# Conditioned mixture of experts and ternary feed-forward on one core: dense experts in two blocks of eight, expert-sorted tokens through DRAM in the other six

## The chip, the cores and the metric

The kernel runs on one core of a Trainium2 chip. The metric is the device time of one launch in microseconds (us). The core has TensorE (PE; its weight loads are shown apart as PEld), VectorE (DVE), ScalarE (ACT), GpSimd (POOL) and SyncE (SP), which here only issues DMAs. Each engine works through its own instructions in the order in which the program was written, and waits on semaphores for the others.

## The reference

4096 tokens (B = 128 rows of S = 32) of width D = 128. Cut to what matters:

```python
U = (mu @ W_dec + b_dec).reshape(B, IN_DIM + 1, K)          # K = 30, one matrix per row of the batch
param = einsum('bik,kj->bij', U, V)                         # rank 30
out = einsum('bsd,bde->bse', x, param[:, :-1]) + param[:, -1:]
gate = out @ Wg.T + bg                                      # 8 experts
topk_scores, topk_idx = top_k(gate, 2);  w = softmax(topk_scores)
h = gelu(einsum('td,ehd->teh', out, W1) + b1)               # H = 256 for each expert
o = einsum('teh,eoh->teo', h, W2) + b2
x = x + (the two chosen experts' o, weighted with w)
c = conditioning(x, ids, states)   # layernorms with table look-ups, one more layer, layernorm
h = silu(tlin(c, w1) * w1_s) * (tlin(c, w2) * w2_s)         # 128 -> 512, weights in {-1, 0, 1}
h = gelu(tlin(h, h1) * h1_s);  h = gelu(tlin(h, h2) * h2_s) # 512 -> 512, twice
x = x + tlin(h, w3) * w3_s                                  # 512 -> 128
```

Only two of the eight experts enter the sum of a token. `out` has rank 30 before the experts, so a token can be carried as 30 numbers and a one (KZ = 32), and the kernel folds V into W1.

## The kernel before, in words

The tokens are cut into eight blocks of TB = 512 (NB = 8). Weights lie in SBUF from the start. PSUM has five kinds of 128x512 tile: `tp` (two), `mm` (two), `ff` (two), `bc` and `acc` (one each).

**Setup.** L184 makes the per-row matrices, `conditioned(i)` (L221) a block's 32 numbers per token (`z4s[i]`, split into two float32r halves), L206 and L207 fold V into W1 (`w4`), L308 computes the gates of all blocks, and `routing` (L252) finds the best two experts by reductions on DVE, and writes their weights as rows (`hot4`, last written in L301).

**`experts(i)`** (L473) runs all eight experts over all 512 tokens of a block. After four transposes of `hot4` (L480) and the bias product (L487), each expert has one matmul that spreads its weights over the partitions (`pbc`, L491), and twice: first layer (`ph`, L495, float32r), gelu on ACT (`hs`, L497), product with the weights on DVE (`hw`, L499) and second layer (`po`, L500, float32, which the profile shows as two matmul records each). Then x is added (L505) and the block is stored to DRAM (`kept_x`, L506) for the case at the end.

**`conditioning(i)`** (L511) is a serial chain: transposes (L522), layernorm x, transposes (`pxh`), table look-ups as matmuls (L542), layernorm h, three products with tables (L559), transposes, five matmuls into `pi` (L576 to L580), a tanh, one more layer (L594, L596), layernorm c, transposes, result `cT`, stored to DRAM (L609). A layernorm (L394) has its statistics and its scaling on DVE and between them two small POOL operations: add eps (L402) and power -0.5 (L403). For layernorm h the scaling itself (L405) is on POOL.

**`feed_forward(i)`** (L631) multiplies in float32r with each activation split into two halves by `halves` (L617): `hi` a cast on ACT (L620), `lo` a subtraction on POOL (L622). Four steps of the gated layer (`pf`; ACT L627, DVE L628 and L629), four of `pgb`, four of `pgc` (matmuls L638, gelu L666), the last layer `pf`, then x is added (L677), four transposes (L680), a copy (L682) and the store.

**Other streams.** `feed_forward_weights` (L360) loads the ternary weights in eleven pieces into five buffers (`ffr`), casts each on ACT, compares on DVE (L368) and sums on POOL (`unequal`, L369) whether a cast changed anything; `count_unequal` puts the sum into a register, and the general path behind it (L748, L749) runs only if it isn't zero. `second_layer_weights` (L422) runs three small state networks, each with a layernorm (`rs_st`).

**Order.** All are generators, and the order in which instructions are written is the order on every engine. `beside` (L51) mixes streams by their share done; L735 to L744 give the stages:

```python
    beside((experts(0), 18), (feed_forward_weights(), 11), (second_layer_weights(), 8))
    count_unequal()
    beside((conditioning(0), 13), (experts(1), 18))
    for i in range(NB):
        streams = [(feed_forward(i), 14)]
        if i + 1 < NB:
            streams.append((conditioning(i + 1), 13))
        if i + 2 < NB:
            streams.append((experts(i + 2), 18))
        beside(*streams)
```

So six stages hold feed-forward i, conditioning i+1 and experts i+2; the seventh has no experts, the eighth is feed-forward 7 alone.

Of the kernel before, what the change touches and what calls it, by code (L numbers as in the profile page):

```python
# [30 lines left out]
VPW = 125  # L31
EPS = 1e-5
# [18 lines left out]
def beside(*streams):  # L51


    left = [[s, n, 0] for s, n in streams]
    while left:
        e = min(left, key=lambda e: (e[2] + 0.5) / e[1])
        e[2] += 1
        if next(e[0], e) is e:
            left.remove(e)
# [3 lines left out]
def adaln_ffn_kernel(ctx: ExitStack, tc: tile.TileContext, a, out: bass.AP):  # L63
# [32 lines left out]
    def rows(tag, n):  # L96

        t = const.tile([P, n], F32R, tag=tag, name=tag)
        nc.gpsimd.memset(t.bitcast(F32), 0.0)
        return t  # L100
# [12 lines left out]

    early = ctx.enter_context(ExitStack())
    setup = early.enter_context(tc.tile_pool(name="setup", bufs=1))
# [10 lines left out]
    x_all = setup.tile([D, NB, TB], F32, tag="x_all", name="x_all")  # L126
    for i in range(NB):
        nc.sync.dma_start(x_all[:, i, :], a["x_t"][:, i * TB : (i + 1) * TB])
    tabs = load("tabs", [4 * E, NTAB], eng=nc.scalar, pool=setup)
    vecs = load("vecs", [P, NVEC], eng=nc.scalar)  # L130
    w2_t = load("moe_w2", [P, E, NH, D])
# [24 lines left out]
    def stacked(dst, src, r, tmp):  # L156
# [3 lines left out]
        hi = tmp.tile([n, dst.shape[1]], F32R, tag="hi", name=f"hi_{dst.tensor.name}", bufs=2)  # L160
# [8 lines left out]
    twice = const.tile([2 * KZ, 2, 2 * KZ], F32R, tag="twice", name="twice")  # L169
# [30 lines left out]
    w4 = const.tile([P, E * H], F32R, tag="w4", name="w4")  # L200
    g4 = const.tile([P, E], F32R, tag="g4", name="g4")

    def folded(dst, w, bias, name):
        n = dst.shape[1]
        pv = ps_acc(name)
        nc.tensor.matmul(pv[:, :n], pre[:, V4 : V4 + P], w, start=True, stop=False)  # L206
        nc.tensor.matmul(pv[:, :n], bias_at, bias, start=False, stop=True)  # L207
        stacked(dst, pv[:, :n], 64, setup)

    def folded_all():  # L210
        folded(g4, pre[:, WG : WG + E], bias_rows[:, E * H :], "pgv")
        yield
        for c in range(E * H // TB):
            cols = slice(c * TB, (c + 1) * TB)
            folded(w4[:, cols], w1_t[:, cols], bias_rows[:, cols], f"pwv_{c}")
            yield


    z4s = [const.tile([P, TB], F32R, tag=f"z4_{i}", name=f"z4_{i}") for i in range(NB)]

    def conditioned(i):  # L221
        xT = x_all[:, i, :]
# [9 lines left out]
        zT = setup.tile([KZ, TB], F32, tag="zT", name=f"zT_{i}", bufs=2)  # L232
# [6 lines left out]
        zh = setup.tile([2 * KZ, TB], F32R, tag="zh", name=f"zh_{i}", bufs=2)  # L239
# [607 lines left out]
```

## Time and profile before

| what | us |
|---|---|
| median of three runs (565.28 to 568.62) | 567.3 |
| the profiled execution | 565.48 |
| its span (first to last instruction) | 563.4 |
| `pwT` of block 0 begins (setup done) | 63.4 |
| x1T of block 0 is stored | 102.1 |
| the output of block 0 is stored | 196.75 |
| outputs of blocks 1 to 5 are stored | 253.25, 309.73, 366.24, 422.75, 479.01 |
| output of block 6 | 522.2 |
| last matmuls of block 7 | 558.4 |

The span is 2.1 us below the profiled execution's time, which is 1.8 us below the median. A stage with three streams takes 56.5 us. All DMAs are issued from the queues of SP and ACT; POOL issues none. The mean granted clock of TensorE is 0.942.

How to read it: the page's first part gives the busy time of each engine, its second part cuts the span into 40 slices of 14.1 us, and its groups give for a line of code how often it ran, the mean of one, and how long its engine sat idle before it and for whom. The table of windows gives the same busy times for stretches of the span, with the clock that was granted to TensorE.

### The profile page before, as it was taken

The page shows a single profiled execution, that of the slowest core. Times are in us where ns is not written, and L with a number is a line of the kernel's source. Part 1 is how long each engine was busy: PE and PEld are TensorE (multiplying, and loading weights), DVE is VectorE, ACT ScalarE, POOL GpSimd, SP SyncE. Part 2 cuts the span into 40 slices and gives each one's busy share as a digit, 9 for nine tenths or more (in the row PEclk, how much of TensorE's full clock was granted, in tenths as well). Part 3 has the DMA queues.
Part 4 walks back from the last instruction along what each step waited for, and adds up shares of the span by engine and source line. Part 5 has one row for each costly group of instructions (what it writes and reads, how often), then busy time and mean ns, then how long its engine had stood idle before and what let it go on. Part 6 is the DMA issues. An engine that isn't in the chain of part 4 may idle for free. (4 is left out here: it accounts for less than half of the span.)

```text
span 563.4 us, 5941 instructions
## 1 busy us (share of the span) xinstructions
PE 497.5 (88%) x1997; PEld 310.3 (55%) x1997; DVE 289.0 (51%) x689; ACT 235.4 (42%) x412; POOL 209.4 (37%) x226
## 2 busy tenths in 40 slices
PE   5998587979899979997999799979997999689694
PEld 5963243534566546654665466546654665365373
DVE  2875786744763565356535653565356535623400
ACT  0141553322455344534453455345534552353343
POOL 3000065030373237323722372237223722384353
PEclk9985599989899999999999999999999999899588
DMA  8800330100100020002000200020001000100100
GB/s 209 298 11 3 113 110 1 39 19 5 53 19 2 2 74 19 0 3 74 19 1 3 74 19 0 5 74 18 1 1 57 0 1 1 56 0 1 37 0 24
DMA packets 14634, 20.46 MB, mean 36 GB/s; under 512 B 1632, under 2 KB 7358, under 8 KB 14342
## 3 DMA queue, kind: packets, MB, share of 16 engines
q1 hardware_dynamic: 13762, 19.56, 10.9%
q10 hardware_dynamic: 836, 0.47, 0.4%
q8 instruction: 18, 0.29, 0.2%
q14 instruction: 18, 0.14, 0.1%
HBM read 13.72 MB, written 6.29 MB: 36 GB/s over the span
## 5 line engine op out<-in xcount | busy, mean ns | idle before, releaser
L500 PE MATMUL po<-hw,moe_w_sb 128*128 128x512 f32 x256 | 135.8, 627 | 8.7 <-DVE hw L499 8.7
L499 DVE TENSOR_TENSOR hw<-hs,pbc 128x512 f32<-128x512 f32 x128 | 85.9, 681 | 67.7 <-PE pbc L491 35.0
L497 ACT ACTIVATE hs<-ph 128x512 f32<-128x512 f32 x128 | 74.6, 596 | 55.2 <-PE ph L495 31.8
L622 POOL TENSOR_TENSOR gc_lo<-gc,gc_hi 128x512 fp32r<-128x512 f32 x32 | 40.7, 1273 | 95.8 <-ACT gc_hi L620 95.2
L500 PEld LDWEIGHTS po<-hw,moe_w_sb 128*128 128x128 f32 x256 | 44.2, 193 | 48.4 <-DVE hw L499 36.5
L622 POOL TENSOR_TENSOR ga_lo<-ga,ga_hi 128x512 fp32r<-128x512 f32 x32 | 41.0, 1280 | 68.9 <-ACT ga_hi L620 68.9
L495 PE MATMUL ph<-z,w 128*128 128x512 f32 x128 | 53.2, 442 | 2.5 <-ACT hs L497 2.5
L622 POOL TENSOR_TENSOR gb_lo<-gb,gb_hi 128x512 fp32r<-128x512 f32 x32 | 40.5, 1287 | 18.8 <-ACT gb_hi L620 16.6
L638 PE MATMUL pgc<-gb_lo,f_h_hi 128*128 128x512 f32 x128 | 44.8, 454 | 1.4 <-POOL gb_lo L622 1.3
L638 PE MATMUL pgb<-ga_hi,f_h_hi 128*128 128x512 f32 x128 | 42.7, 447 | 1.3 <-DVE sl L628 1.3
L666 ACT ACTIVATE gb<-pgb,vecs_sb 128x512 f32<-128x512 f32 x32 | 22.0, 689 | 50.1 <-PE pgb L638 50.1
L638 PE MATMUL pgc<-gb_hi,f_h_hi 128*128 128x512 f32 x128 | 41.0, 437 | 0.1
L666 ACT ACTIVATE gc<-pgc,vecs_sb 128x512 f32<-128x512 f32 x32 | 22.0, 689 | 45.4 <-PE pgc L638 45.4
L627 ACT ACTIVATE sl<-pf,half_w1s 128x512 f32<-128x512 f32 x32 | 22.0, 688 | 43.8 <-PE pf L638 41.1
L638 PE MATMUL pf<-cT_hi,f_w_hi 128*128 128x512 f32 x64 | 32.8, 534 | 8.3 <-DVE sl L628 5.9
L638 PE MATMUL pgb<-ga_lo,f_h_hi 128*128 128x512 f32 x128 | 39.4, 422 | 0.1
L491 PE MATMUL pbc<-w_rows,pick 128*128 128x512 f32 x64 | 36.9, 577 | 0.0
L628 DVE SCALAR_TENSOR_TENSOR sl<-sl,pf 128x512 f32<-128x512 f32 x32 | 21.7, 679 | 20.5 <-ACT sl L627 20.3
L638 PEld LDWEIGHTS pgb<-ga_hi,f_h_hi 128*128 128x128 f32 x128 | 24.8, 196 | 12.9 <-issue 4.1
L638 PEld LDWEIGHTS pgc<-gb_lo,f_h_hi 128*128 128x128 f32 x128 | 24.1, 188 | 13.9 <-issue 6.0
L495 PEld LDWEIGHTS ph<-z,w 128*128 128x128 f32 x128 | 24.9, 196 | 12.1 <-ACT hs L497 6.5
L638 PE MATMUL pf<-cT_lo,f_w_hi 128*128 128x512 f32 x64 | 27.8, 442 | 3.7 <-POOL cT_lo L622 3.6
(230 smaller groups left out, 810.2 us busy)
## 6 DMA issues: line engine op xcount, KB each, us to landing
moe_w_sb<-in_moe_w_dram SPq DMA_DIRECT2D x2, 1024.0 KB
x_all<-in_x_t_dram SPq DMA_DIRECT2D x8, 256.0 KB
xT<-in_x_t_dram SPq DMA_DIRECT2D x8, 256.0 KB
f_h_raw<-in_f_h_dram SPq DMA_DIRECT2D x8, 256.0 KB
kept_x<-x1T SPq DMA_DIRECT2D x8, 256.0 KB
kept_c<-cT SPq DMA_DIRECT2D x8, 256.0 KB
out_dram<-o SPq DMA_DIRECT2D x8, 256.0 KB
pid<-in_pid_dram SPq DMA_DIRECT2D x8, 250.0 KB
```

The lines of the kernel that those rows point to most:

```text
L491: nc.tensor.matmul(pbc, pick[:, e, :], wr, start=True, stop=True)
L495: nc.tensor.matmul(ph, w4[:, c : c + P], z4, start=True, stop=True)
L497: nc.scalar.activation(hs, ph, AF.Gelu)
L499: nc.vector.tensor_tensor(hw, hs, pbc, ALU.mult)
L500: nc.tensor.matmul(po, w2_t[:, e, h, :], hw, start=False, stop=(e == E - 1 and h == NH - 1))
L622: nc.gpsimd.tensor_tensor(lo, src, hi, ALU.subtract)
L627: nc.scalar.activation(tmp, p1, AF.Tanh, scale=half_w1s[:, f : f + 1])
L628: nc.vector.scalar_tensor_tensor(tmp, tmp, 1.0, p1, ALU.add, ALU.mult)
L638: nc.tensor.matmul(dst, w[:, c, f * P : (f + 1) * P], src[c][h], start=(k == 0), stop=(k == len(terms) - 1),)
L666: nc.scalar.activation(t, ph, AF.Gelu, scale=col(s + f))
```

## The change

Blocks 0 and 1 stay dense (ND = 2). For blocks 2 to 7 (NS = 6) each token makes two rows, one for each chosen expert. All 6144 rows are sorted by expert: each expert's rows begin at a multiple of TS = 256, so 31 tiles of 256 rows (NT_S) hold any distribution. There are seven parts.

1. Setup: the gates come from `zT` in float32 inside `conditioned`; blocks 2 to 7 keep their 32 numbers per token with tokens on the partitions (`z_tok`), as halves side by side. `w4` is also stored to DRAM.
2. `sorting`: 24 matmuls rank each row within its expert, 24 count; small DVE operations give each row its place (`row_best`) and each tile its expert (`tile_expert`).
3. `z_rows` in DRAM (7936 rows of 256 bytes) is filled with zeros by one DMA, and 48 indirect DMAs from POOL, of 128 rows each, scatter the tokens into it.
4. `sorted_expert(t)`: the expert's number goes into an SP register; five loads from SP (`w4`, `w2` and `b2` of that expert, the tile's rows twice) and one store; two transposes, two first-layer matmuls (128x256, float32r), one gelu (128x512), four second-layer matmuls (128x128, float32); three DVE operations. Three tiles are in flight.
5. `combined(i)`: x by a load, eight indirect gathers from POOL, eight DVE operations that weight and add, transposes, a copy on ACT and the store to `kept_x`.
6. `in_order` replaces `beside`: each stream has a start and a duration in units of its own, and the steps are sorted by time.
7. The scaling of layernorm h goes from POOL to DVE.

In the order of the instructions that results, POOL has all 48 scatters ahead of the sums into `unequal` and ahead of `rs_st`. PE has `experts(0)` and the first five `ph` of `experts(1)` ahead of the first matmul that needs `rs_st`. SP has all 31 loads of tile numbers in one run. Feed-forward 0 and 1 and conditioning 1 lie among the 31 tiles, conditioning 2 behind them.

```diff
+ND = 2
+NS = NB - ND
+TS = 256
+NT_S = NS * TB * 2 // TS + E - 1
...
-def beside(*streams):
...
+def in_order(*streams):
+    times = [(t + d * k / n, j) for j, (t, d, n, _) in enumerate(streams) for k in range(n)]
+    for _, j in sorted(times):
+        next(streams[j][3], None)
...
+                nc.sync.dma_start(w4_kept[e], w4[:, e * H : (e + 1) * H].bitcast(F32))
...
+        pr = ps_mm("p_rank")
+        nc.tensor.matmul(pr[:, : n * E], before, flat, start=True, stop=False)
+        for d in range(1, n):
+            nc.tensor.matmul(
+                pr[:, d * E : n * E], ones_r, flat[:, : (n - d) * E], start=False, stop=(d == n - 1)
+            )
+        pn = ps_tp("p_count")
+        for c in range(n):
+            nc.tensor.matmul(
+                pn[:, :E], ones_r, flat[:, c * E : (c + 1) * E], start=(c == 0), stop=(c == n - 1)
+            )
...
+    z_rows = kept.tile([NT_S * TS, 2 * KZ], F32, tag="z_rows", name="z_rows")
+    nc.scalar.dma_start(
+        z_rows.rearrange("(p c) k -> p c k", p=P),
+        zeros.unsqueeze(1).to_broadcast([P, n_fill, 2 * KZ]),
+    )
...
+    for c in range(NS * NC):
+        for j in range(2):
+            scatter = nc.gpsimd.indirect_dma_start(
+                z_rows,
+                bass.IndirectOffsetOnAxis(ap=row_best[j][:, c : c + 1], axis=0),
+                z_tok[c // NC][:, c % NC].rearrange("p r k -> p (r k)").bitcast(F32),
+                None,
+            )
...
-    def layernorm(dst, src, n, name, eng=None):
+    def layernorm(dst, src, n, name):
...
-            (eng or nc.vector).tensor_scalar(
+            nc.vector.tensor_scalar(
...
+    def sorted_expert(t):
+        e = nc.values_load(
+            tile_expert[0:1, t : t + 1], engines=[mybir.EngineType.SP], min_val=0, max_val=E - 1
+        )
+        w4_f = exp.tile([P, H], F32, tag="w4_f", name=f"w4_f{t}")
+        nc.sync.dma_start(w4_f, w4_kept[bass.ds(e, 1)].rearrange("o p n -> (o p) n"))
+        w2_e = exp.tile([P, NH * D], F32, tag="w2_e", name=f"w2_e{t}")
+        nc.sync.dma_start(w2_e, a["moe_w2"][bass.ds(e, 1)].rearrange("o p n -> (o p) n"))
+        b2_e = exp.tile([P, D], F32, tag="b2_e", name=f"b2_e{t}")
+        nc.sync.dma_start(b2_e, a["moe_b2"][bass.ds(e, 1), :].partition_broadcast(P))
+        zr = exp.tile([P, TS // P, 2, 2 * KZ], F32, tag="zr", name=f"zr{t}")
+        z_here = z_rows[here].rearrange("(p c) k -> p c k", p=P)
+        for r in range(2):
+            nc.sync.dma_start(zr[:, :, r, :], z_here)
+        w4_e = exp.tile([P, H], F32R, tag="w4_e", name=f"w4_e{t}")
+        nc.vector.tensor_copy(w4_e, w4_f)
...
+        nc.sync.dma_start(y_rows[here].rearrange("(p c) d -> p c d", p=P), y)
...
+    def combined(i):
+        x1 = work.tile([P, NC, D], F32, tag="x1", name=f"x1_{i}", bufs=2)
+        nc.sync.dma_start(x1, a["x"][toks].rearrange("(c p) d -> p c d", p=P))
+        for c in range(NC):
+            for j in range(2):
+                nc.gpsimd.indirect_dma_start(
+                    yg,
+                    None,
+                    y_rows,
+                    bass.IndirectOffsetOnAxis(ap=row_best[j][:, sc : sc + 1], axis=0),
+                )
+                nc.vector.scalar_tensor_tensor(
+                    x1[:, c, :], yg, w_best[j][:, ch : ch + 1], x1[:, c, :], ALU.mult, ALU.add
+                )
...
-    beside((experts(0), 18), (feed_forward_weights(), 11), (second_layer_weights(), 8))
-    count_unequal()
-    beside((conditioning(0), 13), (experts(1), 18))
...
+    in_order(
+        (0.0, 1.0, 18, experts(0)),
+        (0.0, 1.0, 11, feed_forward_weights()),
+        (0.0, 1.0, 8, second_layer_weights()),
+        (1.0, 0.1, 1, count_unequal()),
+        (1.0, 1.0, 18, experts(1)),
+        (1.0, 0.9, 13, conditioning(0)),
+    )
+    dense_stack.close()
+    exp = inner.enter_context(tc.tile_pool(name="exp", bufs=3, side="right", reuse_waits="tile"))
+    in_order(
+        (2.0, 1.2, NT_S + 2, sorted_experts()),
+        (2.0, 0.9, 13, conditioning(1)),
+        (2.0, 1.1, 14, feed_forward(0)),
+        (3.1, 1.2, 14, feed_forward(1)),
+        (3.3, 0.7, 15, conditioning(2)),
+        *((i + 0.9, 0.9, 15, conditioning(i)) for i in range(3, NB)),
+        *((i + 2.3, 1.0, 14, feed_forward(i)) for i in range(2, NB)),
+    )
```

## The prediction

> **What bounds it.** I read the page's header first, then the windows by stage, then single rows. The header names one bound: TensorE.
>
> ```profile
> PE 497.5 (88%) x1997; PEld 310.3 (55%) x1997; DVE 289.0 (51%) x689; ACT 235.4 (42%) x412; POOL 209.4 (37%) x226
> ...
> L500 PE MATMUL po<-hw,moe_w_sb 128*128 128x512 f32 x256 | 135.8, 627 | 8.7 <-DVE hw L499 8.7
> L499 DVE TENSOR_TENSOR hw<-hs,pbc 128x512 f32<-128x512 f32 x128 | 85.9, 681 | 67.7 <-PE pbc L491 35.0
> ```
>
> The largest group (L500) is dense expert work, three quarters of it for experts that a token did not choose. But an average hides stages, so here are the windows (length, then busy time and count of PE, PEld, DVE, ACT, POOL, then granted clock, DMA share, GB/s). First setup, then block 1's experts with conditioning 0, a full stage, the stage without experts, the last feed-forward alone.
>
> ```profile
> 42.00:56.00 14.00, 11.56 (x21) 4.84 (x20) 7.04 (x18) 2.47 (x5) 0.00 (x0) 0.50 0.01 3
> 102.00:144.00 42.00, 35.49 (x114) 17.89 (x112) 23.99 (x65) 12.69 (x24) 6.97 (x10) 0.95 0.10 32
> 309.70:366.20 56.50, 52.79 (x200) 33.12 (x198) 29.24 (x70) 26.19 (x48) 23.22 (x23) 1.00 0.08 25
> 479.00:522.20 43.20, 35.51 (x138) 23.33 (x137) 18.58 (x52) 18.04 (x29) 23.25 (x23) 0.96 0.05 19
> 522.20:563.00 40.80, 29.45 (x92) 19.12 (x92) 6.53 (x10) 16.50 (x27) 16.62 (x13) 0.75 0.07 21
> ```
>
> A full stage has PE busy 93% of 56.5 us: PE-bound. Without experts the stage falls only to 43.2, with PE busy 82%; feed-forward 7 alone still takes 36 us (522.2 to 558.4). So removing expert work helps until the serial chain of a feed-forward is the bound. That is the heart of the case: the gain is capped, and everything new must fit into it.
>
> **PE prices.** Matmul records overlap, so I take the pitch from starts of the timeline (start, us):
>
> ```profile
> 541.77 1.10 PE L638 MATMUL pgb<-ga_lo,f_h_hi 128*128 128x512 f32 x4
> 542.71 1.09 PE L638 MATMUL pgb<-ga_hi,f_h_hi 128*128 128x512 f32 x4
> ```
>
> Four in 0.94 us: 0.235 each. The second expert layer in float32 has two records, so 0.93 for 128x512. Dense experts of a block: 25 float32r products x 0.233 + 16 x 0.93 + 0.6 of transposes = 21.3 us; six blocks lose 128. A sorted tile: two transposes 0.33 (four took 0.67 at the end of the span), two 128x256 products 0.23, four float32 128x128 products 4 x 0.23 = 0.93: 1.5 us; 31 tiles 46.5. Net 81 us of PE less. Feed-forward is 88 float32r matmuls, 20.5 us; conditioning 9.4.
>
> **What indirect DMAs cost POOL.** The trace has no DMA issued from POOL. Call the time of one on POOL's queue c. Bounds by the nearest rows:
>
> ```profile
> 16.05 0.84 SPq L93 DMA_DIRECT2D int_w_sb<-in_int_w_dram  x1
> 16.93 1.00 SPq L93 DMA_DIRECT2D wide_w_sb<-in_wide_w_dram  x1
> ...
> 102.14 0.33 SPq L506 DMA_DIRECT2D kept_x<-x1T  x1
> ```
>
> ```profile
> L369 POOL TENSOR_TENSOR unequal<-unequal,f_h_raw 128x512 f32<-128x512 f32 x8 | 11.5, 1435 | 2.6 <-DVE f_h_raw L368 2.3
> ...
> L403 POOL TENSOR_TENSOR rs_c<-rs_c,mhalf 128x4 f32<-128x4 f32 x8 | 8.2, 1028 | 0.6
> ```
>
> A plain issue is 0.33, issues of many short pieces 0.84 and 1.00; POOL's dearest full operation is 1.44, and a 128x4 power, where hardly any data moves, 1.03. An indirect DMA is an issue of 128 pieces with an address each, so it is nearest to 0.84, 1.00 and 1.03: I take c = 0.95, ends 0.33 and 1.44.
>
> The Trainium skill speaks against the change here. "DMA: Bandwidth & Descriptors", section on the anatomy of one DMA on the gpsimd path, fits 2.0 us plus bytes/436e3 for each; 32 KB gives 2.07, an estimate, and 48 scatters one after the other 99 us, 54 more than at my c. "SBUF — State Buffer", section on who interferes with whom, adds that a two-port DVE copy locks GpSimd out of writing descriptors. No row here shows either. The nearest row is a 256 KB load from SP, issued at 76.23 and cast at 78.85 while further loads were already issued: that latency did not hold the queue.
>
> **The sum along the new order** (span of the changed kernel).
>
> - Setup to the first scatter, 72. Before, `pwT` began at 63.4 after L301. The 48 small rank and count matmuls at the half clock of setup (0.50 in the first window) are about 7, a dozen small DVE rows of 0.25 to 0.4 about 4; the DVE work on `hot4` shrinks to a quarter, -2. The zero fill (7936 packets; on the page q10's 836 packets take 0.4% of 16 x 563.4 us, 43 ns each, so 21 us on 16 engines) is issued by ACT in the first 10 us, and setup hides it; uncovered it costs up to 21. The stores of `w4` are eight SP issues of 0.33 in an idle SP.
> - 48 scatters, 48c = 45.6, to 117.6. The dense experts of block 0 run beneath them (38 us before), so about c = 0.7 is the floor below which this part gains nothing. But `rs_st` and the sums into `unequal` stand behind the scatters on POOL; the `ffr` buffers free only with those sums; and PE stands, in order, at the `pst` transposes that need `rs_st`. So PE and with it the rest of block 1 wait.
> - State networks and weight pieces after that, 20: eleven sums x 1.3 to 1.44 on POOL = 15, and the last chain behind it. On SP the 31 register loads stand ahead of the later weight pieces; at 0 to 0.45 (an issue) they take up to 14, beside the scatters. Before, this ran under experts 0, `rs_st` from 73.8 to 96.0.
> - Rest of experts 1 and conditioning 0, 38 (42 in the second window, five `ph` already done). To 175.6, where the kernel before was at 144: 32 lost.
> - Sorted phase, 113. PE: 46.5 + feed-forward 0 20.5 + feed-forward 1 without its end 18 + conditioning 1 9.4 = 94.4; at 87% busy, between the 93% and 82% of the windows, 109; first tile's loads and filling the pipeline 4. Beside it SP: six DMAs and a register load a tile at 0.33 to 0.45, some 2.7 us, 84 in all; DMA 1024 packets a tile at 43 ns over 16 engines 2.75 us, 85. Both hidden under 3.6 us of PE a tile. At q1's 71 ns (13762 packets, 10.9%) it is 4.5 a tile, 140: no cover then.
> - Conditioning 2 stands behind the last tile, with PE nearly empty: 29 for the last store and the serial chain (28 us of steps), and about 15 gathers on the path, since POOL's order has those of blocks 2 to 5 among its layernorms: 29 + 15c = 43.3. To 331.9.
> - Five blocks at 36.5. PE needs 30 a block, the feed-forward chain 36 (the last window). Conditioning is offset and fills its waits. Gathers (8c = 7.6) and POOL's 13 `lo` x 1.28 = 16.6 fit in a period, hidden. Layernorm h on DVE takes 3.2 us (4 x 0.80) off POOL; DVE has room (43% in the stage without experts). 182.5, to 514.4.
> - Feed-forward 7 alone 36, store and end 5: **555.4**.
>
> That is 495.5 + 63c. The span before was 563.4 and the profiled execution 565.5, so the sum gives 557.5 against 565.5; the median lies 1.8 higher, so **559.3** against 567.3, 1.4% faster. All times below are on the median's scale. 0.5% is about what a measurement of this kernel can tell from no change: below 564.5 is faster, above 570.1 slower.
>
> So of 81 us of PE the change gives back 32 before the sorted phase, 43 in conditioning 2, where PE idles, and the chain's cap takes more.
>
> **Rivals.**
>
> 1. The forecast, c from 0.8 to 1.1: 550 to 569. 0.36.
> 2. Cheap descriptors. c at 0.7 or below hides the scatters under experts 0 (-16), the sorted phase runs at the 93% of a full stage (-7.5), and the period falls to 34.5 since the offsets fill the waits for the gate (-10): **526**. For it: plain issues of 0.33; PE work of 30 us a block. Against: an address for each row. 0.30.
> 3. POOL's queue decides, slower than before. Place: scatters ahead of `rs_st`, then gathers among the layernorms. Price 63 us for each us of c; from c = 1.12 the kernel is over 0.5% slower; at the 1.44 of L369 63 x 0.49 = 31 more, **590**. 0.13.
> 4. Tiles bound by their loads: 4.5 us a tile, 140 for the phase in place of 113, **586**. For it: 17.9 MB move in pieces of 256 bytes to 1 KB through SP alone, three tiles deep. 0.09.
> 5. The later blocks do not get shorter: the offsets change nothing, a block takes the 43.2 of the stage that already has no experts, 5 x 6.7 = 33.5 more, **593**. For it: that row, the same work. Against: there conditioning ends with the stage, so the next feed-forward had to wait; now it ends half a block earlier. 0.12.
>
> **Range and chances.** Below rival 2, c = 0.33 takes 15 x 0.37 = 6 more: 520. Each dear case alone ends at 593 or below, with a little of another at 602; two in full (617 and more) are left out. Range 520 to 602. The forecast's own band splits into faster 0.26, same 0.06, slower 0.04. Faster: 0.26 + 0.30 = 0.56. Same: 0.06. Slower: 0.04 + 0.13 + 0.09 + 0.12 = 0.38.
>
> **What would show it.** The pitch of the scatters on POOL is c, and a PE gap of some 30 us after five `ph` of experts 1, ended by `pst`, shows the stall: no gap means rival 2, a longer one rival 3. The tile pitch in the sorted phase near 3.6 us with PE busy near 87% is right; 4.5 with PE waiting for `zr` or `w4_f` is rival 4. Outputs of blocks 2 to 6 should lie 36.5 apart; 43 is rival 5. Between the last tile and block 2's first `pf` PE should be empty for some 40 us. I would be most wrong if conditioning 2 overlapped the tiles, or if gathers held up the layernorms of every block.

## The result, and the profile after

The changed kernel takes **661.84 us** (median of four runs, 660.86 to 667.46) against 566.3 us (565.28 to 568.62): 1.167 times the kernel before, 95% interval 1.160 to 1.173. It is slower by 95.5 us, where 559.3 was forecast and 602 was the end of the range. The profiled execution is the longest of the four, 667.46 us with a span of 665.6; stage lengths below are its own, of an execution 5.6 us above the median.

The page of the changed kernel: busy time and share by engine, two rows of the 40 slices (16.6 us each), and the queue that POOL feeds.

```profile
PE 474.3 (71%) x2101; PEld 323.6 (49%) x2101; DVE 301.6 (45%) x779; ACT 201.3 (30%) x340; POOL 278.2 (42%) x293
...
PE   6979495223379788888962256775798888889884
...
PEclk9966558655679999999985566788699798989998
...
q0 software_dynamic: 3072, 4.72, 2.8%
```

TensorE was busy 497.5 us and is busy 474.3: the 81 us of work that the prediction took off became 23. Two holes show in the PE row, slices 8 to 11 (116 to 183 us) and 22 and 23 (349 to 383), and the granted clock falls in both and in the setup, so that what runs there runs dearer. The groups of the same page, among them the dense matmul shown of before and the two indirect DMAs:

```profile
L458 POOL DMA_INDIRECT z_rows<-z_tok,row x48 | 46.3, 964 | 100.7 <-DVE row L407 86.3
L650 PE MATMUL po<-hw,moe_w_sb 128*128 128x512 f32 x64 | 41.9, 777 | 42.1 <-DVE hw L649 41.5
...
L737 POOL DMA_INDIRECT yg<-y_rows,row x48 | 47.4, 987 | 43.2 <-DMA y_rows<-y 21.6
L649 DVE TENSOR_TENSOR hw<-hs,pbc 128x512 f32<-128x512 f32 x32 | 21.1, 681 | 63.0 <-remote 52.3
```

The dense matmul (`po`) fell from 256 to 64, but one record costs 777 ns in place of 627. The DVE product ahead of it (`hw`) has 63 us of idle time before it, 52 of them ended by "remote", a release that the trace doesn't trace to an engine; before it waited for PE. Now the same kernel by stages (window; length; busy time and count of PE, PEld, DVE, ACT, POOL; granted clock, DMA share, GB/s): end of setup, the scatters, the state networks, the rest of experts 1 with conditioning 0; then tiles, hole, five feed-forwards, the last one.

```profile
42.00:92.50 50.50, 41.32 (x233) 31.60 (x232) 25.50 (x82) 9.07 (x20) 0.04 (x1) 0.53 0.17 56
92.50:153.10 60.60, 25.68 (x49) 11.31 (x48) 11.70 (x23) 10.54 (x20) 46.24 (x49) 0.70 0.10 30
153.10:187.90 34.80, 14.70 (x42) 8.33 (x42) 14.72 (x28) 6.15 (x13) 16.75 (x17) 0.60 0.22 69
187.90:226.30 38.40, 33.39 (x105) 16.85 (x105) 24.89 (x69) 9.85 (x19) 3.64 (x6) 0.94 0.06 16
```

```profile
226.30:353.30 127.00, 103.42 (x585) 79.87 (x585) 61.30 (x158) 48.92 (x81) 34.66 (x30) 0.96 0.56 152
353.30:410.10 56.80, 20.75 (x61) 12.46 (x62) 25.28 (x84) 5.18 (x10) 38.67 (x42) 0.56 0.22 63
410.10:626.40 216.30, 177.22 (x675) 118.43 (x674) 117.23 (x294) 91.30 (x150) 116.00 (x109) 0.90 0.10 30
626.40:665.00 38.60, 26.50 (x101) 17.09 (x101) 7.17 (x10) 16.80 (x27) 16.70 (x14) 0.94 0.05 16
```

Read the lengths against the PE column. In the 60.6 us of the scatters PE does 25.7, in the 56.8 of the hole 20.8. The five later blocks take 43.3 each with PE busy 35.4. By the prediction's terms the excess falls on these stages:

| stage | forecast | measured | excess |
|---|---|---|---|
| setup to the first scatter | 72 | 92.5 | +20.5 |
| 48 scatters | 45.6 | 60.6 | +15.0 |
| state networks and weights after them | 20 | 34.8 | +14.8 |
| rest of experts 1, conditioning 0 | 38 | 38.4 | +0.4 |
| tiles | 113 | 127.0 | +14.0 |
| last tile to block 2's `pf` | 43.3 | 56.8 | +13.5 |
| five blocks | 182.5 | 216.3 | +33.8 |
| feed-forward 7 and end | 41 | 39.2 | -1.8 |
| span | 555.4 | 665.6 | +110.2 |

One more comparison says why the form itself gains little. From block 0's condition to the last output the kernel before took 414.5 us with PE busy 380.5; after, it is 433 us with PE busy about 328. So 53 us of PE work are gone from this part and it is 19 us longer: PE is no longer what bounds it.

### The profile page after: what moved, and what is told of

It is laid out like the page before. It is cut to its first block, busy times and chain, and to the rows that moved or that the text cites. A ratio compares the mean times of both kernels' runs of the same rounds, so it can differ in the third digit from the quotient of the medians.

```text
span 665.6 us, 6914 instructions
## 1 busy us (share of the span) xinstructions
PE 474.3 (71%) x2101; PEld 323.6 (49%) x2101; DVE 301.6 (45%) x779; ACT 201.3 (30%) x340; POOL 278.2 (42%) x293
## 5 line engine op out<-in xcount | busy, mean ns | idle before, releaser
L458 POOL DMA_INDIRECT z_rows<-z_tok,row x48 | 46.3, 964 | 100.7 <-DVE row L407 86.3
L650 PE MATMUL po<-hw,moe_w_sb 128*128 128x512 f32 x64 | 41.9, 777 | 42.1 <-DVE hw L649 41.5
L872 POOL TENSOR_TENSOR ga_lo<-ga,ga_hi 128x512 fp32r<-128x512 f32 x32 | 40.8, 1276 | 74.1 <-ACT ga_hi L870 71.2
L737 POOL DMA_INDIRECT yg<-y_rows,row x48 | 47.4, 987 | 43.2 <-DMA y_rows<-y 21.6
L872 POOL TENSOR_TENSOR gc_lo<-gc,gc_hi 128x512 fp32r<-128x512 f32 x32 | 41.3, 1296 | 45.1 <-ACT gc_hi L870 43.5
L872 POOL TENSOR_TENSOR gb_lo<-gb,gb_hi 128x512 fp32r<-128x512 f32 x32 | 41.3, 1291 | 38.2 <-ACT gb_hi L870 38.0
L649 DVE TENSOR_TENSOR hw<-hs,pbc 128x512 f32<-128x512 f32 x32 | 21.1, 681 | 63.0 <-remote 52.3
L888 PE MATMUL pgb<-ga_lo,f_h_hi 128*128 128x512 f32 x128 | 40.8, 421 | 3.1 <-POOL ga_lo L872 3.1
L888 PE MATMUL pgb<-ga_hi,f_h_hi 128*128 128x512 f32 x128 | 42.3, 432 | 0.7 <-DVE sl L878 0.7
L647 ACT ACTIVATE hs<-ph 128x512 f32<-128x512 f32 x32 | 18.9, 597 | 78.9 <-DVE hw L649 27.9
L650 PEld LDWEIGHTS po<-hw,moe_w_sb 128*128 128x128 f32 x64 | 13.9, 238 | 57.1 <-DVE hw L649 49.3
L699 PE MATMUL py<-w_e,hss 128*128 128x128 f32 x248 | 37.3, 292 | 2.4 <-ACT hss L694 1.8
L699 PEld LDWEIGHTS py<-w_e,hss 128*128 128x128 f32 x248 | 32.6, 200 | 10.5 <-ACT hss L694 8.6
L916 ACT ACTIVATE gb<-pgb,vecs_sb 128x512 f32<-128x512 f32 x32 | 22.0, 687 | 43.2 <-PE pgb L888 38.9
L878 DVE SCALAR_TENSOR_TENSOR sl<-sl,pf 128x512 f32<-128x512 f32 x32 | 21.7, 679 | 22.8 <-ACT sl L877 22.5
L694 ACT ACTIVATE hss<-phs 128x512 f32<-128x512 f32 x31 | 18.5, 598 | 42.2 <-PE phs L690 42.0
L888 PEld LDWEIGHTS pgb<-ga_lo,f_h_hi 128*128 128x128 f32 x128 | 24.7, 194 | 10.8 <-POOL ga_lo L872 5.9
```

Of the source, the lines that this page charges most:

```text
L458: scatter = nc.gpsimd.indirect_dma_start(z_rows, bass.IndirectOffsetOnAxis(ap=row_best[j][:, c : c + 1], axis=0), z_tok[c // NC][:, c % NC ...
L647: nc.scalar.activation(hs, ph, AF.Gelu)
L649: nc.vector.tensor_tensor(hw, hs, pbc, ALU.mult)
L650: nc.tensor.matmul(po, w2_t[:, e, h * D : (h + 1) * D], hw, start=False, stop=(e == E - 1 and h == NH - 1))
L694: nc.scalar.activation(hs.rearrange("p h t -> p (h t)"), ph, AF.Gelu)
L699: nc.tensor.matmul(py[:, c * D : (c + 1) * D], hs[:, h, c * P : (c + 1) * P], w2_e[:, h * D : (h + 1) * D], start=(h == 0), stop=(h == NH ...
```

## The experiments

The theory after the result: four independent costs (scatters and what they hold up, tile loads, gathers ahead of block 2, a period that the chain sets). Each run takes out one. Times are to be set beside 661.84; stage lengths beside the table. Single times are of one execution unless an interval stands with them.

### Register loads or scatters: what stops DVE and ACT

After the first ten scatters or so, DVE and ACT of the changed kernel work only in short bursts. DVE's timeline between 109 and 162 us (start, length, operation, idle time before it) has nothing but these four lines, and a window in between is empty on three engines:

```profile
109.65 1.28 DVE L649 TENSOR_TENSOR hw<-hs,pbc 128x512 f32<-128x512 f32 x2 [5.54 <-remote]
123.80 1.29 DVE L649 TENSOR_TENSOR hw<-hs,pbc 128x512 f32<-128x512 f32 x2 [12.87 <-remote]
142.71 1.29 DVE L649 TENSOR_TENSOR hw<-hs,pbc 128x512 f32<-128x512 f32 x2 [17.61 <-remote]
160.24 1.29 DVE L649 TENSOR_TENSOR hw<-hs,pbc 128x512 f32<-128x512 f32 x2 [16.25 <-remote]
```

```profile
132.00:142.00 10.00, 0.00 (x0) 0.00 (x0) 0.00 (x0) 0.00 (x0) 7.56 (x9) 0.50 0.09 26
```

The `hw` at 123.80 needs the gelu that ended at 112.0 and a matmul that ended at 114.3, so it starts 9.5 us after its inputs were there. Two things run at that time on other queues: 48 scatters on POOL and 31 register loads on SP.

**late_regs.** The register loads read a copy that POOL makes behind the scatters.

```diff
+    tile_expert_late = const.tile([1, NT_S], I32, tag="tile_expert_late", name="tile_expert_late")
+    nc.gpsimd.tensor_copy(tile_expert_late, tile_expert)
...
-            tile_expert[0:1, t : t + 1], engines=[mybir.EngineType.SP], min_val=0, max_val=E - 1
+            tile_expert_late[0:1, t : t + 1], engines=[mybir.EngineType.SP], min_val=0, max_val=E - 1
```

> The tiles' expert numbers pass through a POOL copy behind the last scatter, so that SP's 31 register loads come after the scatters instead of beside them; nothing else changes. Theory S (outstanding scatters hold up the instruction starts of ACT, DVE and SP): experts 0 is still drawn out, x1T of block 0 is stored at 150 us or later (168.8 in the changed kernel), the total stays at 655 to 665. Theory R (the register loads hold them up): x1T of block 0 at about 130, the state networks done at about 173 instead of 188, the total at about 646.

Measured 655.81 us. The loads now run from 161.4 to 178.5 us, behind the scatters (87.5 to 147.3), and DVE still stops:

```profile
130.67 1.28 DVE L652 TENSOR_TENSOR hw<-hs,pbc 128x512 f32<-128x512 f32 x2 [16.97 <-remote]
150.27 1.28 DVE L652 TENSOR_TENSOR hw<-hs,pbc 128x512 f32<-128x512 f32 x2 [18.32 <-issue]
```

So the register loads aren't the cause. Where the loads stand alone they follow each other at 0.57 us; beside the scatters of the changed kernel they had taken 2.3 us each on the mean (31 from 92.7 to 162.4).

**no_scatter.** The 48 scatters are left out.

```diff
-    for c in range(NS * NC):
-        for j in range(2):
-            scatter = nc.gpsimd.indirect_dma_start(
...
-            )
-            tc.declare_no_dep(scatter.ins, group="z_rows", reason="rows are distinct")
-            tc.add_to_no_dep_group("z_rows", scatter.ins)
```

> The 48 scatters are left out, so the sorted blocks see rows of zeros; the register loads stay where they are. Theory S: the 31 register loads take 0.57 us each (18 us) instead of 70 us in all, x1T of block 0 at about 130, state networks hidden as in the kernel before, conditioning 0 done at about 165 instead of 226, total about 600. Theory R: register loads still 2 us each, x1T of block 0 at 150 or later, total 620 to 635.

Measured 603.11 us, 59 less. The window from the end of sorting to block 0's condition:

```profile
84.00:162.90 78.90, 69.39 (x201) 35.07 (x200) 54.30 (x128) 28.80 (x52) 22.04 (x23) 0.87 0.14 42
```

78.9 us where the changed kernel has 133.8 (92.5 to 226.3): no stop is left, PE is busy 88%, and its clock is 0.87. The scatters and what they hold up, 55 us here, are the largest single cost, and even without them the kernel is 37 us slower than before.

**late_scatter.** The scatters are written behind experts 0, the weights and the state networks.

```diff
-    for c in range(NS * NC):
-        for j in range(2):
-            scatter = nc.gpsimd.indirect_dma_start(
...
     in_order(
         (0.0, 1.0, 18, experts(0)),
         (0.0, 1.0, 11, feed_forward_weights()),
         (0.0, 1.0, 8, second_layer_weights()),
+    )
+    for c in range(NS * NC):
+        for j in range(2):
+            scatter = nc.gpsimd.indirect_dma_start(
...
+    in_order(
         (1.0, 0.1, 1, count_unequal()),
```

> The scatters are issued after experts 0, the weight pieces and the state networks in the program, so that POOL mixes them with the sums into `unequal` and `rs_st` instead of doing all of them first. Theory S (scatters in flight hold up ACT, DVE and SP, wherever they stand): conditioning 0 ends at 205 to 220 instead of 226, total 640 to 655. Rival (it was their place ahead of `rs_st` on POOL, as the prediction had it): conditioning 0 ends at 185 to 195, total about 625.

Measured 643.24 us. In the built program the scatters don't stand behind the sums and `rs_st` on POOL but mixed with them, so the written order, which the description of the kernel takes as the order on every engine, isn't kept here. They run from 95.3 to 171.5, at a pitch of 1.62, and block 0's condition is done at 206.4, 20 us sooner. No stop of DVE ended by "remote" shows (ACT has two, 4.6 us together); in its place DVE waits for POOL's turn:

```profile
DVE st_hat L542 <- POOL rs_st L540: 25.6, 3, 11.7
```

(Total wait, number, longest.) So the queue was hidden only in part, and the wait of the prediction, `rs_st` behind scatters, is what is late next.

**spaced_scatter.** A POOL addition of 128x512 stands behind each scatter.

```diff
+    spacer = filled([P, TB], 0.0, "spacer")
+    nc.vector.tensor_copy(spacer[:, : NS * NC], row_best[1])
...
             tc.add_to_no_dep_group("z_rows", scatter.ins)
+            nc.gpsimd.tensor_tensor(spacer, spacer, spacer, ALU.add)
```

> Behind each scatter POOL does one 128x512 addition on a tile that nobody reads (1.28 us), which doubles the pitch of the scatters to about 2.5 us; they end at about 215. If the hold-up comes from scatters in flight at any rate, ACT and DVE pause through all of that time and x1T of block 0 is stored at 190 or later. If it comes from their rate (a queue that fills), the pauses vanish: x1T of block 0 at about 130, as without scatters. Total 700 to 725 in both, for the state networks wait for the scatters either way.

Measured 700.28 us. DVE's timeline in the same part of the kernel, scatters at a pitch of 2.21 us running from 90.1 on:

```profile
99.17 0.69 DVE L652 TENSOR_TENSOR hw<-hs,pbc 128x512 f32<-128x512 f32 x1 [0.49 <-PE pbc L644]
100.97 0.68 DVE L652 TENSOR_TENSOR hw<-hs,pbc 128x512 f32<-128x512 f32 x1
103.11 1.28 DVE L652 TENSOR_TENSOR hw<-hs,pbc 128x512 f32<-128x512 f32 x2 [0.15 <-PE pbc L644]
106.17 1.28 DVE L652 TENSOR_TENSOR hw<-hs,pbc 128x512 f32<-128x512 f32 x2 [1.78 <-PE pbc L644]
```

The stops are gone: block 0's experts are stored 33 us after their start, where they took 80 in the changed kernel. The total is longer because the train is now 104 us and the state networks wait for `rs_st` at its end, 83.7 us in one wait.

It is tempting to conclude that a train of scatters stops the other engines when it has no pauses, but a run that comes below for another reason, merged_loads, speaks against it. It has the same 48 scatters with nothing between them, at the same pitch of 1.26 us (103.9 to 163.9), and the register loads beside them (0.63 us each). DVE in that run:

```profile
125.93 1.28 DVE L654 TENSOR_TENSOR hw<-hs,pbc 128x512 f32<-128x512 f32 x2 [1.77 <-PE pbc L646]
129.00 1.28 DVE L654 TENSOR_TENSOR hw<-hs,pbc 128x512 f32<-128x512 f32 x2 [1.78 <-PE pbc L646]
131.77 0.69 DVE L660 TENSOR_TENSOR x1T<-po,xT 128x512 f32<-128x512 f32 x1 [1.48 <-PE po L655]
168.05 0.41 DVE L560 TENSOR_SCALAR st_hat<-pst,mv_st,rs_st 128x128 f32<-128x128 f32 x1 [35.59 <-POOL rs_st L558]
```

No stop at all: block 0's experts are done 33 us after their start, beneath the train, and then DVE waits for `rs_st` behind the scatters, as the prediction said. From the first scatter on that run has (same columns as the stages above):

```profile
103.90:164.50 60.60, 25.23 (x62) 11.65 (x61) 14.96 (x28) 12.99 (x24) 46.26 (x48) 0.73 0.13 39
164.50:188.40 23.90, 8.63 (x29) 5.83 (x29) 12.28 (x23) 4.06 (x9) 17.57 (x18) 0.50 0.26 79
188.40:227.80 39.40, 34.66 (x105) 17.65 (x105) 24.84 (x68) 9.80 (x18) 3.64 (x6) 0.88 0.06 19
```

That is 123.9 us against 133.8 in the changed kernel and 78.9 in no_scatter. So of the 55 us only about 10 go to the stops; some 45 are the pitch and the queue, `rs_st` and the sums behind 48 scatters. The stops need the scatters, since no_scatter has none, but the scatters alone don't make them.

### Gathers

**plain_gathers.** Each indirect gather becomes a plain load of 128 rows, issued by SP.

```diff
-                nc.gpsimd.indirect_dma_start(
-                    yg,
-                    None,
-                    y_rows,
-                    bass.IndirectOffsetOnAxis(ap=row_best[j][:, sc : sc + 1], axis=0),
-                )
+                nc.sync.dma_start(yg, y_rows[NT_S * TS - P :])
```

> Each indirect gather becomes a plain load from SP of the last 128 rows of the experts' output, so the sums take wrong rows, but wait for the last tile as before; the scatters stay. Theory G (POOL's gathers, 1.25 us each, stretch the later blocks and conditioning 2): the outputs of blocks 2 to 6 lie 37 us apart instead of 43, the gap from the last tile to block 2's feed-forward falls from 57 to 42, total about 620. Theory P (the order of feed-forward and conditioning on PE sets the period): the period stays at 40 or more, total 645 to 655.

Measured 625.67 us, 36 less. The hole, last tile to block 2's first `pf`:

```profile
343.20:383.30 40.10, 20.00 (x60) 12.09 (x61) 24.49 (x84) 5.18 (x9) 7.37 (x10) 0.62 0.29 90
```

40.1 in place of 56.8, with POOL at 7.4 in place of 38.7. The waits in the hole of the changed kernel name the same chain:

```profile
POOL yg L737 <- DMA y_rows<-y: 21.6, 1, 21.6
...
PEld px L563 <- DVE x L743: 14.7, 4, 7.7
DVE x L743 <- DMA yg<-y_rows,row: 14.0, 12, 5.2
```

The hole is the serial part (about 40, forecast 29) and the gathers, some 17 on the path (forecast 15c = 14). Another 14 came from the first feed-forward behind it: the outputs of blocks 1 and 2 lie 40.8 apart where they were 54.9. In the changed kernel POOL still does gathers there (until 464.5), and PE waits 8.8 us for `gc_lo`, which is also POOL's work. The later period stays at 38.6 to 41.1, where it was 38.5 to 42.3: gathers aren't what sets it.

### Tile loads

In the tiles of the changed kernel PE and DVE wait for loads:

```profile
PE pzr L680 <- DMA zr<-z_rows: 15.3, 15, 2.4
...
DVE w_e L677 <- DMA w_f<-w_kept: 14.5, 10, 2.4
```

**one_load_per_expert.** The expert of a tile is fixed, and its weights are loaded once for all its tiles.

```diff
-        e = nc.values_load(
-            tile_expert[0:1, t : t + 1], engines=[mybir.EngineType.SP], min_val=0, max_val=E - 1
-        )
...
+        e = t * E // NT_S
+        if e not in held:
...
+            held[e] = (w4_e, w2_e, b2_e)
+        w4_e, w2_e, b2_e = held[e]
```

> Tiles take fixed experts, tile t the expert t*8/31, and an expert's three weight tiles are loaded and copied once instead of once for each tile (24 loads instead of 93, no register loads); the rows are still loaded per tile, so the outputs of the sorted blocks use wrong experts. Theory L (loads and SP's issues stretch the tile phase, where PE waits 15 us for rows): the phase from conditioning 0 to the last tile falls from 127 to about 112. Rival (PE and the chains of feed-forward 0 and 1 set it): 122 or more.

Measured 620.84 us, 41 less:

```profile
210.70:296.60 85.90, 78.70 (x517) 67.17 (x517) 49.27 (x132) 37.54 (x65) 22.65 (x21) 0.98 0.49 137
```

85.9 us in place of 127, PE busy 92%. Part of feed-forward 1 now lies behind the last tile and fills the hole, which is why PE's own work in the window is 25 less too, so not all of the 41 is waiting that is gone.

**merged_loads.** The whole computation, with a tile's weights in one load and its rows in one: three DMAs a tile, where there were six, for the same bytes.

```diff
-    w4_kept = kept.tile([E, P, H], F32, tag="w4_kept", name="w4_kept")
+    NW = H + NH * D + D
+    w4_kept = kept.tile([E, P, NW], F32, tag="w4_kept", name="w4_kept")
+    nc.scalar.dma_start(w4_kept[:, :, H : H + NH * D], a["moe_w2"])
...
+        w_e = exp.tile([P, NW], F32, tag="w_e", name=f"w_e{t}")
+        nc.sync.dma_start(w_e, w4_kept[bass.ds(e, 1)].rearrange("o p n -> (o p) n"))
...
-        for r in range(2):
-            nc.sync.dma_start(zr[:, :, r, :], z_here)
+        nc.sync.dma_start(
+            zr, z_here.unsqueeze(2).to_broadcast([P, TS // P, 2, 2 * KZ])
+        )
```

> Changed kernel, but each tile's weights come by one load in place of three (first layer, second layer and its bias lie side by side in one kept record of 640 columns, still picked by the register), and the sorted rows by one load in place of two: three transfers per tile on SP's queue where there were six, with the same bytes. Theory L (SP's queue, six transfers per tile issued one after the other, is what sets the tile pitch): the tile phase falls from 127 us to about 95 (86 with the loads of 23 tiles left out, plus what three issues leave), total about 625 to 635. Rival (the bytes, or the latency between y's store and the next load, set it): phase 115 to 127, total 650 to 667. Nothing else should move: scatters still about 60 us, later outputs still 38 to 42 us apart.

Measured 645.58 us, ratio 1.137 (1.130 to 1.145) to the kernel before.

```profile
227.80:327.00 99.20, 89.02 (x534) 71.41 (x535) 59.59 (x158) 42.51 (x71) 26.82 (x24) 0.97 0.69 193
```

The tiles take 99.2 us, near the 95 expected, with as many bytes and 193 GB/s in place of 152, so the bytes weren't the bound. Here too some of feed-forward 1 has moved behind the last tile (PE's work in the window is 14 less), and 4 of the 28 us come back there. Merging also made the pieces of the weights larger (35278 packets in the tiles became 25612), but the time that the DMA engines were busy hardly changed, 71 us (0.56 of 127) and 68 (0.69 of 99.2): it wasn't the bound either. Whether SP's issues were (six a tile, then three) or the wait from a load to its landing, no run separates. The total missed its 625 to 635 since the copies that build the records stand ahead of the setup's own loads, and the first scatter came at 103.9.

### The setup

**setup_order.** The folding of V into W1 goes behind the last conditioned block, with seven buffers for the loads of x.

```diff
-        x_t.append(setup.tile([D, TB], F32, tag="x_t", name=f"x_t{i}", bufs=4))
+        x_t.append(setup.tile([D, TB], F32, tag="x_t", name=f"x_t{i}", bufs=7))
...
-        (1.5, 6.0, 4, folding),
+        (8.0, 1.0, 4, folding),
```

> The four folding steps of W1 come after the last conditioned block instead of between them, and x has seven buffers in setup instead of four; nothing else changes. Theory F (the folding steps and the waiting loads keep the gates back): the gates are done at about 53 instead of 69, the first scatter starts at about 77 instead of 92.5, total about 646. Rival: the gates' own float32 matmuls on a half clock set it, the first scatter starts at 87 or later, total over 655.

Measured 655.24 us. The gates are done at 57.6 (68.7 before the edit), but the folding then stood ahead of the ranking, and the first scatter came at 84.8. Kernels of this study whose setup is not edited have it between 86.3 and 95.3, so the order is worth a few us at most. What is left is the setup's own work at about half clock, 41.3 us of PE in the first window above, at 0.53; no run takes it out.

### The offset alone

**dense_offset.** The kernel before, all blocks dense, with the new offsets and layernorm h on DVE.

```diff
-        layernorm(h1, h1, NC, f"h_{i}", eng=nc.gpsimd)
+        layernorm(h1, h1, NC, f"h_{i}")
...
-    for i in range(NB):
-        streams = [(feed_forward(i), 14)]
...
+    in_order(
+        *((float(i), 1.0, 18, experts(i)) for i in range(1, NB)),
+        *((i + 1.0, 0.6, 13, conditioning(i)) for i in range(NB)),
+        *((i + 1.6, 1.0, 14, feed_forward(i)) for i in range(NB)),
+    )
```

> One part of the change alone: all eight blocks stay dense, no sorting, no indirect DMA; the streams are offset in time (experts i from i, conditioning i from i + 1.0 for 0.6, feed-forward i from i + 1.6 for 1.0) and layernorm h is scaled on DVE. Theory O (PE stays the bound and the offsets shorten only the end, where 43 + 36 us become 28 + 36): 545 to 558, the full stages still 56 us apart. Rival (the offset order makes PE wait for conditioning inside the full stages): stages over 58 us, total over 570.

Measured 577.47 us, ratio 1.017 (1.014 to 1.020). A full stage:

```profile
194.40:252.60 58.20, 54.37 (x200) 33.17 (x198) 32.42 (x75) 26.75 (x47) 20.27 (x19) 0.97 0.07 23
```

58.2 us with PE at 93%, where the stage shown of before has 56.5 at 93%: with PE full, the offset has nothing to fill. PE's own time is 1.6 more here, at a clock of 0.97; in a stage at 1.00 (310.7 to 367.6) it is 53.1 of 56.9 us. The end got longer and not shorter: the last outputs lie 52.5 and 42.7 apart, 43.7 and 35.8 before. What the offset does for stages without experts this run doesn't separate.

### All remedies together

**combined.** Merged loads; the scatters as a stream of 48 steps over both dense blocks, an addition behind each; the sums of unequal weights, half of the low halves of the hidden layers and those of the condition on DVE; feed-forward 1 0.2 of a stage ahead, and feed-forward 0 and conditioning 1 a tenth of a stage shorter.

```diff
+    in_order(
+        (0.0, 2.0, 2 * NS * NC, scatters()),
         (0.0, 1.0, 18, experts(0)),
...
-                nc.gpsimd.tensor_tensor(unequal, unequal, raw.rearrange("p c o -> p (c o)"), ALU.add)
+                nc.vector.tensor_tensor(unequal, unequal, raw.rearrange("p c o -> p (c o)"), ALU.add)
...
+        eng = nc.vector if on_dve else nc.gpsimd
+        eng.tensor_tensor(lo, src, hi, ALU.subtract)
...
+                dst.append(halves(t, "f", f"{name}_{i}_{f}", 8, f % 2 == 1))
```

> The remedies that the runs so far point to, together, with the whole computation done: tile loads merged (as in the other run), the scatters spread as a stream of 48 steps with a POOL addition of 256 columns behind each over both dense blocks, the counting of unequal weights on DVE, half of the low halves of the FF hidden layers and those of the condition on DVE, FF 1 moved 0.2 of a stage ahead. If the losses add up (scatter hold-up and its wait 30 to 45, tile loads 30 to 40, the hole ahead of block 2 about 10, period 40 to 38): 570 to 595 us, still not under the kernel before (566). Rival (the losses cover each other, so that one freed only uncovers the next): 605 to 640. Under 560 would say that the sorted form pays once its four costs are taken out.

Measured 606.45 us, ratio 1.068 (1.062 to 1.075): just inside the rival's 605 to 640. Two things weren't as meant. The additions depend on nothing late, so they ran during the setup, and the pitch of the scatters was 1.3; and the first scatter came at 106.5, as in merged_loads.

**combined_late.** The copies go behind the fill of `z_rows`, the scatters are written from half a stage in, behind most of the state networks, and the additions are dropped.

```diff
-    nc.scalar.dma_start(w4_kept[:, :, H : H + NH * D], a["moe_w2"])
...
+    nc.scalar.dma_start(w4_kept[:, :, H : H + NH * D], a["moe_w2"])
...
-        (0.0, 2.0, 2 * NS * NC, scatters()),
+        (0.5, 1.5, 2 * NS * NC, scatters()),
...
-        (0.0, 1.0, 8, second_layer_weights()),
+        (0.0, 0.6, 8, second_layer_weights()),
```

> The combined kernel with two things moved: the two copies that build the merged weight records are issued behind the fill of the sorted rows (in the combined kernel they stood ahead of the setup's own loads, and the first scatter came at 106 us in place of 92), and the scatters are a stream that begins half a stage in, behind the state networks, with no addition behind each. Theory that the losses add: the setup gives back about 12 us and the state networks no longer wait 34 us for POOL, of which the scatters' own length leaves 0 to 15: 580 to 595 us. Rival (they cover each other): 600 to 606, as the combined kernel. Neither is expected under 566.

Measured **590.08 us**, ratio 1.044 (1.039 to 1.050). It is the fastest sorted version here, and still 24 us over the kernel before. The built program again keeps another order than the written one: POOL starts with nine scatters, the `rs_st` of the three networks stand among the others (103.7, 128.3 and 145.9), and DVE still waits 22.8 us for two of them. Its stages, dense blocks with scatters first:

```profile
91.80:197.90 106.10, 72.37 (x199) 36.19 (x197) 55.38 (x129) 28.01 (x52) 55.22 (x60) 0.80 0.22 64
197.90:295.10 97.20, 87.36 (x538) 69.91 (x538) 63.51 (x165) 42.29 (x71) 19.61 (x19) 0.98 0.70 197
295.10:352.50 57.40, 33.46 (x112) 22.25 (x110) 29.02 (x88) 12.90 (x21) 40.88 (x44) 0.76 0.22 62
352.50:548.80 196.30, 167.82 (x672) 117.04 (x672) 120.14 (x320) 91.06 (x147) 84.39 (x84) 0.92 0.10 33
548.80:586.90 38.10, 27.82 (x101) 18.92 (x101) 10.64 (x15) 16.85 (x27) 10.44 (x9) 0.87 0.06 16
```

Against the changed kernel: scatters with dense blocks -27.7, tiles -29.8, hole +0.6, later blocks -20.0, end -1.1; with the setup's -0.7 the 78.7 by which the spans differ. That stages sum to the span is no finding; that the tiles gave back what they gave in merged_loads (27.8), and that no other stage grew by more than 0.6 for it, is what says that the losses add. What is left: the scatters still cost 27 us over no_scatter's 78.9, the hole is untouched, and a block takes 39.3 with PE busy 33.6. With half of `lo` taken from POOL, the outputs of blocks 3 to 6 lie 36.4 to 37.7 apart (38.5 to 40.0 in the changed kernel), and PE's waits for `gc_lo`, 9.7 us in the five blocks, are gone, so POOL's low halves were part of the chain that set 40.

## Why the prediction was wrong

The likeliest single case, the forecast, was wrong in sign, and the reason isn't one price: almost every term was low, and cases that were listed as alternatives held together.

- **"Range and chances".** This is the step that failed first. Each dear case was given its own time, "alone", and two in full were left out as too unlikely. But rival 3 (POOL's queue), rival 4 (loads) and rival 5 (the period) sit in different stages and nothing makes one exclude another. By the table they came to +28.5 (scatters and hole), +14 and +34 at once. The runs confirm that they add: taking out scatters, gathers and weight loads one by one gave 59, 36 and 41, and combined_late got 72 from remedies in different stages.
- **"Take c = 0.95".** The record of a scatter lasts 0.964 us, as chosen, but the next follows 0.30 later: pitch 1.26, inside the bounds 0.33 and 1.44. The rows from which it was read gave the length of an issue, not the distance between two. By the prediction's own formula c = 1.26 alone makes 578.8 us, past the point (1.12) from which rival 3 decides.
- **"The dense experts of block 0 run beneath" the scatters, and "state networks and weight pieces after that, 20".** In the changed kernel this cover failed: experts 0 were stored 80 us after their start in place of 39, PE waited for `hw` before it ever stood at `pst`, and the networks took 34.8 instead of 20. But the mechanism was right: where the stops don't come (merged_loads) the experts do run beneath the scatters, PE then stands 36.3 us at `pst`, and the networks take 23.9. So of the +14.8 about 11 are the stops, which nothing in the prediction foresaw and whose cause stays open, and 4 a low price.
- **"Setup to the first scatter, 72".** 92.5. Gates in float32 and the folding in front of the last conditioned blocks kept the gates until 68.7 (47.7 before), ranking and counting took 10.2 where 7 was priced, and routing no longer lies under the folding.
- **"Sorted phase, 113 ... both hidden".** 127. PE's work was sized low (94.4 against 103.4 busy), and the loads were not hidden: one_load_per_expert and merged_loads show 86 and 99 with fewer transfers. Rival 4 had the stage right (loads) and its size by packets (140) too high. Its reason, small pieces through SP, holds at most in part: the engines' time for the pieces hardly changed (71 and 68 us) when the same bytes went in half the transfers and the tiles ended 28 us sooner.
- **"29 + 15c".** The count of gathers was right, 17 us on the path by plain_gathers; the serial part is 40, not 29.
- **"Five blocks at 36.5. PE needs 30 a block", gathers "hidden".** 43.3 on the mean. That this is rival 5's 43.2 is luck: the outputs of blocks 1 and 2 lie 54.9 apart, and those after them 40.2 on the mean. So two steps failed. The gathers aren't hidden in the first of these blocks, where they cost 14 (plain_gathers), and the period is 40.2 for 36.5, part of it POOL's low halves. The warning was on the page: the window of the stage without experts, shown in the prediction, has PE busy 35.51 us for this very work. The 30 came from the pitch of matmuls in a dense run at full clock, and was preferred to the row. Busy PE is 35.4 a block now, at a clock of 0.90, and 33.6 in combined_late, at 0.92; at 36.5 a block that would be PE busy 92 to 97%.
- **Net 81 us of PE less.** 23 on the whole span. From block 0's condition on it is 53; the other 30 went into the setup (72.7 us of PE to the first scatter, at a clock of 0.73; before, 49.0 to `pwT`) and into dense work at a clock of 0.60 to 0.70. A `po` record costs 777 ns on the mean.

What held: rest of experts 1 and conditioning 0 (38.4), feed-forward 7 (39.2 with the end, for 41), the hole behind the tiles (foreseen, 13.5 longer), and that the gain would be capped by the chain.

On the rules that were set against the change. The Trainium skill, "DMA: Bandwidth & Descriptors", section on the anatomy of one DMA on the gpsimd path: its fit made 48 scatters 99 us, an estimate. They took 60.6 at their own pace, so 2.07 us is not what one costs the queue. As the time from issue to landing it agrees: in combined that is 2.1, 2.2 and 4.2 us (least, median, most), and the next scatter is issued before it is over. The lock of the Trainium skill's "SBUF — State Buffer" (section on who interferes with whom) doesn't show: the scatters of merged_loads kept 1.26 whether DVE worked or stood. But what DVE did beside them was nearly all TENSOR_TENSOR and not copies, so no run here tests it.

## What to carry to other kernels

Price a stage from the window that already holds the same work, with its clock, before any sum of pitches; where the two differ, start from the window. Ask of every pair of rivals whether one excludes the other: costs in different stages add, and the range must hold their sum. And removing work from the bounding engine pays only until the next chain: here each cost had to be taken out by itself, and with most of them gone the sorted form was still 4% behind dense work that kept TensorE at 93% in its full stages.

## What the hardware showed that was not expected

- In the changed kernel, a train of 48 indirect scatters (128 rows of 256 bytes) at a pitch of 1.26 us had beside it ACT, DVE and SP's register loads starting only now and then, from about the tenth scatter on: DVE's next operations came 5.5, 12.9, 17.6 and 16.3 us after the last ones, SP's steps were mostly multiples of about 0.70 us apart, and this lasted until 7 us after the last scatter. PE and POOL showed none of it. Without scatters it is gone, at 2.21 us too, and the register loads aren't needed for it (late_regs). But the same train at 1.26 us in merged_loads shows none of it, so the scatters are needed and don't suffice. A backlog of the transfers themselves is not it: the trace of the changed kernel has no DMA traffic at all from 154.5 to 163 us, and DVE stood until 160.24. The cause stays open.
- Six small transfers a tile from one queue gave 152 GB/s, three larger ones for the same bytes 193, and a tile's share of the phase, with the other work among the tiles, fell from 4.1 to 3.2 us (127 and 99.2 over 31).
- A hole costs twice: in windows with PE idle half the time or more the granted clock was 0.50 to 0.70, and dense matmul records went from 627 to 777 ns on the mean.
